# Row sums of an attention kernel: the first head's exponentials interleaved and summed on VectorE, three heads added on GpSimd

## The chip, the core and the metric

The kernel runs on one core of one Trainium2 chip. The metric is the device time of one execution in microseconds (us). Five engines work side by side and meet through semaphores: TensorE (PE, its weight loads are shown as PEld), VectorE (DVE), ScalarE (ACT), GpSimd (POOL) and SyncE (SP), which here only starts transfers.

## The reference

One block of a diffusion transformer on `x` of 2 x 2048 x 512 with a condition of 2 x 512. The condition makes six shifts, scales and gates; attention is causal over 2048 tokens with 16 heads of 32; a GELU layer of width 2048 follows.

```python
scores = jnp.einsum('bhqd,bhkd->bhqk', q, k) * scale
causal = jnp.tril(jnp.ones((t, t), bool))
scores = jnp.where(causal, scores, -jnp.inf)
attn = jax.nn.softmax(scores, axis=-1)
out = jnp.einsum('bhqk,bhkd->bhqd', attn, v)
...
mod = jax.nn.silu(condition) @ Wada + bada
sh_a, sc_a, gt_a, sh_m, sc_m, gt_m = jnp.split(mod, 6, axis=1)
xm = _layernorm(x, g1, be1) * (1.0 + sc_a[:, None, :]) + sh_a[:, None, :]
x = x + gt_a[:, None, :] * _attention(xm, Wqkv, Wproj, bproj)
xm = _layernorm(x, g2, be2) * (1.0 + sc_m[:, None, :]) + sh_m[:, None, :]
h = jax.nn.gelu(xm @ W1 + b1, approximate=False)
x = x + gt_m[:, None, :] * (h @ W2 + b2)
```

The softmax is exact: its maximum over the keys is subtracted, and its sum over the keys divides. The change concerns that sum.

## The kernel before, in words

The two rows of the batch are worked one after the other: projections to q, k and v, then attention, then the output projection; a Strassen-like multilayer stage for both rows closes the run. Everything is f32, with scores in the f32r form.

Attention of one row is cut into 16 units, `units`: four column blocks `c` of four heads each (`HC` = 4, 32 columns a head), and in each block four blocks `i` of 512 queries (`QB`, `TQ` = 4 tiles of 128). In block 0 they run in the order 0, 1, 2, 3, in the others 0, 2, 1, 3. A unit goes over its key tiles of 128 in steps: 4 i steps for tiles wholly below the diagonal, one for the first diagonal tile, one for the second and fourth together, one for the third (`steps_of`, line 662).

A step does this, in the order in which the code writes it; nearly all instructions keep that order on their engine (`mm`, `act`):

- `scores_t` (line 550): for four heads PE writes minus the row maxima into four banks (`st<-fold,sel`), adds the transposed scores, keys by queries (`st<-qst,kst`), and ACT takes the exponential of each into `e` (line 593). On diagonal tiles POOL zeroes what lies above the diagonal (line 602). There are four `st` banks.
- Between these, PE makes scores the other way round, queries by keys, for units up to three ahead (`score`, `bank`; `s<-kst,qst`), and DVE takes their row maxima (`mx`, lines 461 and, on the diagonal with a causal mask, 456). They use two `s` banks, and one score in a step borrows an `st` bank. How many are made in a step is set by `due` from fixed costs. When a unit's last maximum is there, `split` (lines 478 to 482) and `rows` (line 522) form the rows that the next unit's first matmuls need. In the last unit of a row no scores are left to make.
- `flush` runs what was put off: `values` (`o<-e,vv`) two steps later (`LAG`), and the row sums `sm`, matmuls of `e` or of a chain of sums with a matrix of ones.
- The row sums are not taken of every tile. For each group of four full key tiles the four `e` of the same head are first added, by POOL or, in the last unit of a row, by DVE (`add`, line 621), and one matmul per head then sums the result over the keys. The last group of a unit takes in the first diagonal tile as well. The other diagonal tiles go straight to PE.

The four heads of a step lie in two tiles of two heads each, so an add is one instruction of 1024 elements a partition for two heads. There is room for four steps of `e` and for two chains.

Of the kernel before, what the change touches and what calls it, by code (L numbers as in the profile page):

```python
# [8 lines left out]
F32 = mybir.dt.float32  # L9
F32R = mybir.dt.float32r  # L10
BF16 = mybir.dt.bfloat16
AF = mybir.ActivationFunctionType
ALU = mybir.AluOpType
AX = mybir.AxisListType
# [3 lines left out]
P = 128  # L18
H = 16
HD = 32  # L20
EPS = 1e-5
QB = 512
# [5 lines left out]
def dit_block_kernel(  # L28
# [36 lines left out]
    nc = tc.nc  # L65
# [5 lines left out]
    HC = P // HD  # L71
    TQ = QB // P
# [4 lines left out]
    E_BUFS = 16  # L77
    EE_BUFS = 8
# [5 lines left out]
    def pool(name, bufs=1, **kw):  # L84
# [5 lines left out]
    bp = bp_cm.__enter__()  # L90

    ident = const.tile([P, P], F32, tag="ident", name="ident")
# [2 lines left out]
    causal = bp.tile([P, QB], BF16, tag="causal", name="causal")  # L95
    nc.gpsimd.memset(causal[:, : QB - P], 0.0)
    make_causal_mask(nc, causal[:, QB - P :], mask_val=MASKED)
    ones = bp.tile([P, P], F32, tag="ones", name="ones")
    nc.gpsimd.memset(ones, 1.0)
    eps = const.tile([P, 1], F32, tag="eps", name="eps")  # L100
    nc.gpsimd.memset(eps, EPS)
# [2 lines left out]
    sel = bp.tile([P, P], BF16, tag="sel", name="sel")  # L104
    ident_h = bp.tile([P, P], BF16, tag="ident_h", name="ident_h")
    nc.vector.tensor_copy(ident_h, ident)
    nc.vector.tensor_scalar(sel, ones, -1.0, None, ALU.mult)
    tmask = bp.tile([P, TQ + 1], F32, tag="tmask", name="tmask")
    nc.vector.tensor_reduce(
        tmask[:, :TQ],  # L110
# [1 line left out]
        axis=AX.XY,  # L112
        op=ALU.add,
# [21 lines left out]
    first = const.tile([P, 1], F32, tag="first", name="first")  # L135
# [65 lines left out]
    def mm(*args, **kw):  # L201

        return tc.keep_in_program_order(nc.tensor.matmul(*args, **kw))  # L203

    def act(ins):

        return tc.keep_in_program_order(ins)
# [81 lines left out]
    class Row:  # L289


        def __init__(self, b):
            self.b = b
            self.vv = bp.tile([P, NT, D], F32, tag="vv", name="vv")
            self.kst, self.qst, self.pools = {}, {}, {0: bp}
            self.at = 0
            self.todo = [
                (u, h, t, kb)
                for u, (_, i) in enumerate(units)
                for h in range(HC)  # L300
                for t in range(TQ)
                for kb in range(i + 1)
            ]
            self.mx = None
            self.spent = 0
            self.rows_made = 0
# [234 lines left out]
    def attention_phase(row):  # L541
        b, vv, kst, qst = row.b, row.vv, row.kst, row.qst
        with pool(f"att{b}") as ap, pool(
# [2 lines left out]
            row.pools[1] = ap  # L546

            n_bank = [0]

            def scores_t(u, step, n):  # L550

                def st_bank():  # L560

                    n_bank[0] += u == len(units) - 1
                    if n_bank[0] % 6 >= HC:
                        return ps_sp.tile([P, QB], F32, tag="s", name="st")
                    return ps_stp.tile([P, QB], F32, tag="st", name="st")

                c, i = units[u]
                tiles = steps_of[u][step]
                q0 = tiles[0][1]
                w = sum(QB - q for _, q in tiles)  # L570
                sts, es = [], []
                for h in range(HC):
                    g = slice(h * HD, (h + 1) * HD)
                    st = st_bank()
                    mm(
                        st[:, :w], sel[g, :], fold[u % 2][g, q0 : q0 + w],
                        start=True, stop=False,
                    )
                    sts.append(st)
                for h in range(HC):  # L580
                    at = 0
                    for j, q in tiles:
                        mm(
                            sts[h][:, at : at + QB - q],
                            kst[c][:, h, j * P : (j + 1) * P],
                            qst[u][:, h, q:],
                            start=False, stop=at + QB - q == w,
                        )
                        at += QB - q
                    if h % 2 == 0:  # L590
                        e = ap.tile([P, 2, QB], F32, tag="e", name="e", bufs=E_BUFS // 2)
                        es.append(e)
                    act(nc.scalar.activation(e[:, h % 2, :w], sts[h][:, :w], AF.Exp))  # L593
                    if tiles[0][0] >= i * TQ and (h % 2 or len(tiles) > 1):

                        if len(tiles) > 1:
                            d = e[:, h % 2, :].rearrange("p (t k) -> p t k", k=P)
                            d = d[:, 0 : TQ : TQ - 1, :]
                        else:
                            d = e[:, :, :P]  # L600
                        act(
                            nc.gpsimd.affine_select(  # L602
                                d, d, pattern=[[0, 2], [1, P]],
                                compare_op=ALU.is_ge, fill=0.0,
                                base=0, channel_multiplier=-1,
                            )
                        )
                    if h < 2 and n >= 3 or h >= HC - n and n < 3:
                        row.score(1)
                if n >= 3:  # L610
                    row.score(1, st_bank)
                    row.score(min(n, HC) - 3)
                return es, max(0, n - HC)

            def new_sums():
                return [
                    ap.tile([P, 2, QB], F32, tag="ee", name="ee", bufs=EE_BUFS // 2)
                    for _ in range(HC // 2)
                ]

            def add(u, dst, x, y):
                engine = nc.vector if u == len(units) - 1 else nc.gpsimd
                act(engine.tensor_tensor(dst, x, y, ALU.add))  # L623

            def add_to(u, chain, es):
                for t, e in zip(chain, es):
                    add(u, t, t, e)

            def begin_chain(u, es0, es1):
                chain = new_sums()  # L630
                for t, e0, e1 in zip(chain, es0, es1):
                    add(u, t, e0, e1)
                return chain

            def products(dst, lhs, es, q0, at, first, last):
                for h in range(HC):
                    mm(
                        dst[h * HD : (h + 1) * HD, q0:], lhs(h),
                        es[h // 2][:, h % 2, at : at + QB - q0], start=first, stop=last,
                    )  # L640

            def finish(u, o, sm):
# [26 lines left out]
            for u, (c, i) in enumerate(units):  # L669
                for n, tiles in enumerate(steps_of[u]):  # L670
                    w = sum(QB - q for _, q in tiles)
# [12 lines left out]
            for u, (c, i) in enumerate(units):  # L684
# [5 lines left out]
                for n_step, tiles in enumerate(steps_of[u]):  # L690
                    last = n_step == steps - 1
                    if n_step == 0:
                        summed = set()
                        o = ps_op.tile([P, QB], F32, tag="o", name="o")
                        sm = ps_op.tile([P, QB], F32, tag="sm", name="sm")
# [6 lines left out]
                    if u == 0 and n_step < LAG:  # L702

                        n = max(n, HC)
                    es, rest = scores_t(u, n_step, n)
                    rest = len(row.todo) - rest
                    make_rows = False
# [12 lines left out]
                    def tile_by_tile(dst, lhs, es, tiles, first, last):  # L720
                        at = 0
                        for n, (j, q) in enumerate(tiles):
                            products(
                                dst, lambda h: lhs(j, h), es, q, at,
                                first and n == 0, last and n == len(tiles) - 1,
                            )
                            at += QB - q
# [8 lines left out]
                    def row_sums(es, last, tiles=((0, 0),), sm=sm, summed=summed):  # L736
                        first = not summed
                        summed.add(len(summed))
                        tile_by_tile(sm, lambda j, h: ones[:, :HD], es, tiles, first, last)

                    pending.append((now + LAG, values))
                    sums_of, wait = None, 0
                    if n_step < i * TQ:
                        k = n_step % TQ
                        if k == 0:
                            even = es
                        elif k == 1:
                            chain = begin_chain(u, even, es)
                        else:
                            add_to(u, chain, es)  # L750
                        if k == TQ - 1 and n_step + 1 < i * TQ:
                            sums_of, wait = (chain, False), 2
                    elif i and n_step == i * TQ:
                        add_to(u, chain, es)
                        sums_of, wait = (chain, False), 2
                    else:

                        sums_of, wait = (es, last, tiles), i > 0 and not last
                    if sums_of:
                        pending.append(  # L760
                            (now + LAG + wait, lambda f=row_sums, s=sums_of: f(*s))
                        )
# [304 lines left out]
    with pool("wada") as wp, pool("qkv0") as qp, pool(  # L1067
# [123 lines left out]
        with pool("hl0") as hp:  # L1191
# [8 lines left out]
            quarters.store()  # L1200

    attention_phase(row)


# [720 lines left out]
```

## Time and profile before

| | |
|---|---|
| time, median of 2 runs | 2317.93 us (2315.91 to 2319.94) |
| the profiled execution | 2323.13 us, its span 2321.4 us |
| PE busy | 2270.8 us (98%) |
| DVE busy | 1582.5 us (68%) |
| POOL busy | 1290.9 us (56%) |
| ACT busy | 914.6 us (39%) |
| granted clock of PE, mean | 0.998 |
| POOL, adds of 1024 (line 623) | 212 + 84, 2385 ns each |
| ACT, exponentials of 512 (line 593) | 1024, 603 ns each |

A profile shows one execution. Its page lists the busy time of each engine and the costliest groups of instructions: line, engine, operation, written and read tiles, shapes, count, then busy time and mean duration, then how long the engine stood idle just before them and for whom. Matmuls are pipelined, so their durations overlap and their ends are modelled; the distance from start to start tells their pace. An order of instructions lists start, duration, and in square brackets the idle time before. Attention of the first row fills some 213 to 737 us of the span, that of the second 997 to 1528.

### The profile page before, as it was taken

Reading aid. Unit: us, or ns where it says so; the run is one execution under the profiler, and the core shown is the slowest. Engines: PE = TensorE matmul, PEld = TensorE weight load, DVE = VectorE, ACT = ScalarE, POOL = GpSimd, SP = SyncE. Lnnn points to the kernel's source line nnn. Section 1 sums busy time; section 2 is a strip of 40 time slices with the busy share of each in tenths; the row PEclk is TensorE's granted clock in tenths of the full one; section 3 lists DMA queues with packets and bytes.
Section 4 is the critical chain, followed back from the end, with each engine's and each line's share of the span. In section 5 each row is a group of like instructions: output and inputs, shape, how many; then the busy total and the mean of one; then the engine's idle time right before and its main releaser. Section 6 shows DMA issues by size and latency. Waiting matters only on the chain. (4 is left out here: it accounts for less than half of the span.)

```text
span 2321.4 us, 33398 instructions
## 1 busy us (share of the span) xinstructions
PE 2270.8 (98%) x12141; PEld 1388.8 (60%) x12141; DVE 1582.5 (68%) x3117; ACT 914.6 (39%) x1744; POOL 1290.9 (56%) x1036
## 2 busy tenths in 40 slices
PE   8999999999999999999999999999999999999998
PEld 4455545455544444555455554446888888888887
DVE  3366776777666735677667777555896876877787
ACT  2112555555565021155555554622332152251230
POOL 1052987878793663478788886653764602602510
PEclk9999999999999999999999999999999999999999
DMA  7577216151233799981522404265375554654643
GB/s 257 185 243 204 55 28 133 29 119 47 74 115 127 241 297 298 320 235 24 113 48 48 100 24 134 81 206 205 118 279 200 199 186 146 212 173 151 216 143 116
DMA packets 118524, 355.60 MB, mean 153 GB/s; under 512 B 14496, under 2 KB 15052, under 8 KB 103640
## 3 DMA queue, kind: packets, MB, share of 16 engines
q1 hardware_dynamic: 107040, 293.64, 41.9%
q0 software_dynamic: 10944, 59.28, 7.0%
q8 instruction: 96, 1.57, 0.3%
q14 instruction: 68, 0.56, 0.1%
q10 hardware_dynamic: 376, 0.55, 0.1%
HBM read 253.80 MB, written 107.48 MB: 156 GB/s over the span
## 5 line engine op out<-in xcount | busy, mean ns | idle before, releaser
L593 ACT ACTIVATE e<-st 128x512 f32<-128x512 f32 (+1 forms) x1152 | 573.1, 579 | 411.6 <-PE st L203 350.5
L461 DVE TENSOR_REDUCE mx<-s 128x1 f32<-128x512 f32 x604 | 408.0, 687 | 185.0 <-PE s L203 183.6
L623 POOL TENSOR_TENSOR ee<-ee,e 128x1024 f32<-128x1024 f32 x212 | 498.8, 2385 | 8.3 <-ACT e L593 8.3
L203 PE MATMUL s<-kst,qst 128*128 128x512 f32 (+3 forms) x1032 | 466.5, 453 | 15.9 <-DVE mx L461 6.3
L203 PE MATMUL st<-qst,kst 128*128 128x512 f32 (+3 forms) x1280 | 410.1, 387 | 0.0
L203 PE MATMUL ps_a<-sum,room 128*128 128x256 f32 x1504 | 357.4, 382 | 6.6 <-DVE c L1409 3.8
L203 PEld LDWEIGHTS ps_a<-sum,room 128*128 128x128 f32 x1504 | 281.5, 190 | 56.0 <-issue 8.7
L203 PE MATMUL o<-e,vv 128*32 128x512 f32 (+3 forms) x2560 | 300.8, 539 | 0.8 <-POOL e L602 0.8
L203 PEld LDWEIGHTS s<-kst,qst 128*128 128x128 f32 x1032 | 194.5, 189 | 174.0 <-DVE mx L461 58.6
L456 DVE CUSTOM_DVE_ANT_0 junk<-s,causal 128x512 bf16<-128x512 f32 (+3 forms) x428 | 209.2, 489 | 126.2 <-PE s L203 118.7
L203 PEld LDWEIGHTS st<-qst,kst 128*128 128x128 f32 x1280 | 227.5, 188 | 96.8 <-issue 66.7
L623 POOL TENSOR_TENSOR ee<-e 128x1024 f32<-128x1024 f32 x84 | 198.4, 2384 | 130.5 <-ACT e L593 130.4
L203 PE MATMUL ps_qk<-xmT,wqkv 128*128 128x512 f32 x512 | 240.5, 597 | 1.8 <-DVE xmT L263 1.8
L602 POOL TENSOR_SCALAR_AFFINE_SELECT e<-e 128x256 f32<-128x256 f32 x256 | 103.8, 436 | 107.2 <-ACT e L593 74.2
L203 PEld LDWEIGHTS ps_qk<-xmT,wqkv 128*128 128x128 f32 x512 | 94.2, 190 | 97.7 <-issue 91.4
L1637 POOL TENSOR_TENSOR c<-c,h 128x512 f32<-128x512 f32 x40 | 58.2, 1474 | 160.8 <-ACT c L1635 160.8
L203 PE MATMUL ps_b<-sum,room 128*128 128x256 f32 x608 | 143.6, 379 | 0.0
L203 PEld LDWEIGHTS ps_b<-sum,room 128*128 128x128 f32 x608 | 115.0, 190 | 15.4
L203 PE MATMUL ps_v<-wqkv,xmT 128*128 128x512 f32 x256 | 122.3, 594 | 0.0
L203 PEld LDWEIGHTS o<-e,vv 128*32 128x32 f32 x2560 | 60.8, 108 | 101.1 <-issue 83.4
L203 PE MATMUL st<-fold,sel 32*128 32x512 bf16 (+1 forms) x1152 | 116.1, 372 | 3.6 <-DVE mhl L482 2.6
L461 DVE TENSOR_REDUCE mx<-st 128x1 f32<-128x512 f32 x164 | 112.7, 687 | 4.9 <-PE st L203 2.7
(179 smaller groups left out, 2869.6 us busy)
## 6 DMA issues: line engine op xcount, KB each, us to landing
qst<-q SPq DMA_DIRECT2D x128, 256.0 KB
room<-w1e SPq DMA_DIRECT2D x28, 1024.0 KB
kst<-k SPq DMA_DIRECT2D x24, 1024.0 KB
room<-w1e SPq DMA_DIRECT2D x28, 768.0 KB
room<-w2e SPq DMA_DIRECT2D x21, 1024.0 KB
q<-hl SPq DMA_DIRECT2D x32, 512.0 KB
k<-hl SPq DMA_DIRECT2D x32, 512.0 KB
room<-w2e SPq DMA_DIRECT2D x21, 768.0 KB
```

What stands on the lines that cost most here:

```text
L203: return tc.keep_in_program_order(nc.tensor.matmul(*args, **kw))
L456: nc.vector.tensor_tensor_reduce(junk[:, :w], s[:, :w], causal[:, QB - w :], 1.0, MASKED, ALU.add, ALU.max, m,)
L461: nc.vector.tensor_reduce(m, s[:, :w], axis=AX.X, op=ALU.max)
L593: act(nc.scalar.activation(e[:, h % 2, :w], sts[h][:, :w], AF.Exp))
L602: nc.gpsimd.affine_select(d, d, pattern=[[0, 2], [1, P]], compare_op=ALU.is_ge, fill=0.0, base=0, channel_multiplier=-1,)
L623: act(engine.tensor_tensor(dst, x, y, ALU.add))
L1637: nc.gpsimd.tensor_tensor(c, c, piece_of(base, i, t, pair), ALU.add)
```

## The change

The first of the four heads is taken out of the pairs. Its exponentials of four successive key tiles go into one tile `[P, QB, TQ]`, so that for each query the values of the four key tiles lie side by side: ACT writes them, and PE reads them, at a step of four elements (16 bytes). When the fourth is there, one `tensor_reduce` on DVE over the innermost axis gives the sum of the group for that head, 2048 elements read and 512 written. The other three heads lie side by side in one tile of 3 x 512, and each add is one instruction of 1536. In the last group of a unit, the first diagonal tile of the first head is added by an add of its own. The masking on the diagonal goes by one head and three heads instead of two and two. There is room for two groups of the first head, four steps of the others, and two chains, as before. The matrix of ones shrinks to the 32 columns that are used.

```diff
@@ scores_t and above it
+            four = [None]
+            class Heads:
+                def __init__(self, first, rest):
+                    self.first, self.rest = first, rest
+                def of(self, h):
+                    return self.rest[:, h - 1, :] if h else self.first
+            def exponentials(step):
+                if step % TQ == 0:
+                    four[0] = ap.tile([P, QB, TQ], F32, tag="e0", name="e", bufs=2)
+                return Heads(
+                    four[0][:, :, step % TQ],
+                    ap.tile([P, HC - 1, QB], F32, tag="e", name="e", bufs=E_BUFS // HC),
+                )
...
-                sts, es = [], []
+                sts, es = [], exponentials(step)
...
-                    if h % 2 == 0:
-                        e = ap.tile([P, 2, QB], F32, tag="e", name="e", bufs=E_BUFS // 2)
-                        es.append(e)
-                    act(nc.scalar.activation(e[:, h % 2, :w], sts[h][:, :w], AF.Exp))
-                    if tiles[0][0] >= i * TQ and (h % 2 or len(tiles) > 1):
+                    e = es.of(h)
+                    act(nc.scalar.activation(e[:, :w], sts[h][:, :w], AF.Exp))
+                    if tiles[0][0] >= i * TQ and (h in (0, HC - 1) or len(tiles) > 1):
...
             def add_to(u, chain, es):
-                for t, e in zip(chain, es):
-                    add(u, t, t, e)
+                add(u, chain.rest, chain.rest, es.rest)
             def begin_chain(u, es0, es1):
-                chain = new_sums()
-                for t, e0, e1 in zip(chain, es0, es1):
-                    add(u, t, e0, e1)
+                chain = Heads(
+                    ap.tile([P, QB], F32, tag="ee0", name="ee", bufs=2),
+                    ap.tile([P, HC - 1, QB], F32, tag="ee", name="ee", bufs=2),
+                )
+                add(u, chain.rest, es0.rest, es1.rest)
                 return chain
+            def four_of_first(chain):
+                act(
+                    nc.vector.tensor_reduce(
+                        chain.first, four[0], axis=AX.X, op=ALU.add,
+                    )
+                )
             def products(dst, lhs, es, q0, at, first, last):
...
-                        es[h // 2][:, h % 2, at : at + QB - q0], start=first, stop=last,
+                        es.of(h)[:, at : at + QB - q0], start=first, stop=last,
...
-                        if k == TQ - 1 and n_step + 1 < i * TQ:
-                            sums_of, wait = (chain, False), 2
+                        if k == TQ - 1:
+                            four_of_first(chain)
+                            if n_step + 1 < i * TQ:
+                                sums_of, wait = (chain, False), 2
                     elif i and n_step == i * TQ:
                         add_to(u, chain, es)
+                        add(u, chain.first, chain.first, es.first)
                         sums_of, wait = (chain, False), 2
```

More of the change, by code (lines that the diff above doesn't have):

```diff
@@ L97, in dit_block_kernel @@
     make_causal_mask(nc, causal[:, QB - P :], mask_val=MASKED)
-    ones = bp.tile([P, P], F32, tag="ones", name="ones")
+    ones = bp.tile([P, HD], F32, tag="ones", name="ones")
     nc.gpsimd.memset(ones, 1.0)
@@ L106, in dit_block_kernel @@
     nc.vector.tensor_copy(ident_h, ident)
-    nc.vector.tensor_scalar(sel, ones, -1.0, None, ALU.mult)
+    nc.vector.tensor_scalar(sel, ident, 0.0, -1.0, ALU.mult, ALU.add)
     tmask = bp.tile([P, TQ + 1], F32, tag="tmask", name="tmask")
@@ L589, in scores_t @@
                         at += QB - q
-                    if h % 2 == 0:
-                        e = ap.tile([P, 2, QB], F32, tag="e", name="e", bufs=E_BUFS // 2)
-                        es.append(e)
-                    act(nc.scalar.activation(e[:, h % 2, :w], sts[h][:, :w], AF.Exp))
-                    if tiles[0][0] >= i * TQ and (h % 2 or len(tiles) > 1):
-                        if len(tiles) > 1:
-                            d = e[:, h % 2, :].rearrange("p (t k) -> p t k", k=P)
-                            d = d[:, 0 : TQ : TQ - 1, :]
+                    e = es.of(h)
+                    act(nc.scalar.activation(e[:, :w], sts[h][:, :w], AF.Exp))
+                    if tiles[0][0] >= i * TQ and (h in (0, HC - 1) or len(tiles) > 1):
+                        if h == 0 or len(tiles) > 1:
+                            d = e.rearrange("p (t k) -> p t k", k=P)
+                            d = d[:, 0 : TQ : TQ - 1, :][:, : len(tiles), :]
                         else:
-                            d = e[:, :, :P]
+                            d = es.rest[:, :, :P]
                         act(
                             nc.gpsimd.affine_select(
-                                d, d, pattern=[[0, 2], [1, P]],
+                                d, d, pattern=[[0, d.shape[1]], [1, P]],
                                 compare_op=ALU.is_ge, fill=0.0,
@@ L613, in scores_t @@
                 return es, max(0, n - HC)
[L615 to L619, printed above, removed]
             def add(u, dst, x, y):
@@ L625, in add_to @@
             def add_to(u, chain, es):
-                for t, e in zip(chain, es):
-                    add(u, t, t, e)
+                add(u, chain.rest, chain.rest, es.rest)
             def begin_chain(u, es0, es1):
-                chain = new_sums()
-                for t, e0, e1 in zip(chain, es0, es1):
-                    add(u, t, e0, e1)
-                return chain
+                chain = Heads(
[3 more added lines that the diff above has]
+                add(u, chain.rest, es0.rest, es1.rest)
+                return chain
+            def four_of_first(chain):
+                act(
+                    nc.vector.tensor_reduce(
+                        chain.first, four[0],
+                        axis=AX.X, op=ALU.add,
+                    )
+                )
             def products(dst, lhs, es, q0, at, first, last):
@@ L738, in row_sums @@
                         summed.add(len(summed))
-                        tile_by_tile(sm, lambda j, h: ones[:, :HD], es, tiles, first, last)
+                        tile_by_tile(sm, lambda j, h: ones, es, tiles, first, last)
                     pending.append((now + LAG, values))
```

## The prediction

> **What bounds the kernel now.** I read the page's first part, then the busy table of the four attention stretches (both rows of the batch, without their last unit; then one long unit; then a last unit), then the groups by shape, the waits and the order of instructions. The columns of the busy table are stretch, length, busy time and count for PE, PEld, DVE, ACT and POOL, then the granted clock and the DMA's share and rate.
>
> ```profile
> span 2321.4 us, 33398 instructions
> PE 2270.8 (98%) x12141; PEld 1388.8 (60%) x12141; DVE 1582.5 (68%) x3117; ACT 914.6 (39%) x1744; POOL 1290.9 (56%) x1036
> 213.45:693.84 480.39, 474.08 (x3308) 241.71 (x3308) 335.74 (x840) 272.01 (x545) 388.07 (x262) 1.00 0.33 80
> 996.93:1484.29 487.36, 476.87 (x3308) 242.64 (x3308) 340.28 (x844) 271.94 (x545) 392.14 (x266) 1.00 0.33 84
> 291.02:336.80 45.78, 45.78 (x308) 22.68 (x305) 32.49 (x83) 26.00 (x50) 38.67 (x20) 1.00 0.12 29
> 1484.29:1527.50 43.21, 42.26 (x307) 16.91 (x304) 30.82 (x30) 31.23 (x63) 10.85 (x13) 1.00 0.19 68
> ```
>
> PE sets the pace: it idles 6.3 us in 480.4 and 10.5 in 487.4, at the full granted clock. POOL is busy for 81% of these stretches, DVE for 70%, and in the long unit (third row) for 84% and 71%. So whatever the change takes from POOL can bring at most what PE now loses on account of POOL. That is small:
>
> ```profile
> DVE mx L461 <- PE s L203: 183.6, 279, 2.8
> ACT e L593 <- POOL ee L623: 15.1, 10, 1.7
> ```
>
> All waits of ACT for POOL are 15.1 us in the whole run, and ACT idles for hundreds more. PE's own matmuls wait 0.8 us for POOL's masking (a row further down) and show none for its sums. What PE does lean on is DVE: each score matmul `s` needs one of two banks that DVE's maximum frees. One group of four key tiles in the long unit shows it, PE's rows first, then DVE's (start, length):
>
> ```profile
> 307.06 0.49 PE L203 MATMUL s<-kst,qst 128*128 128x512 f32 x1
> 308.15 0.39 PE L203 MATMUL s<-kst,qst 128*128 128x512 f32 x1
> 308.37 0.39 PE L203 MATMUL st<-qst,kst 128*128 128x512 f32 x1
> 308.60 0.34 PE L203 MATMUL s<-kst,qst 128*128 128x384 f32 x1
> 309.48 0.39 PE L203 MATMUL s<-kst,qst 128*128 128x512 f32 x1
> 309.80 1.07 PE L203 MATMUL o<-e,vv 128*32 128x512 f32 x8
> 310.80 0.40 PE L203 MATMUL st<-fold,sel 32*128 32x512 bf16 x4
> 307.59 0.69 DVE L461 TENSOR_REDUCE mx<-s 128x1 f32<-128x512 f32 x1 [0.51 <-PE s L203]
> 308.57 0.69 DVE L461 TENSOR_REDUCE mx<-s 128x1 f32<-128x512 f32 x1 [0.29 <-PE s L203]
> ```
>
> The step's last score is issued at 307.06 and DVE has its maximum by 308.28. DVE idles 0.29 us and reduces the score of 308.15 by 309.26. PE writes the same bank again at 309.48, only 0.22 us later. DVE is thus not full, but the slack at each bank is tenths of a microsecond.
>
> **The change, part by part.** Durations come from these rows (last numbers before the second bar: busy us, mean ns):
>
> ```profile
> L623 POOL TENSOR_TENSOR ee<-ee,e 128x1024 f32<-128x1024 f32 x212 | 498.8, 2385 | 8.3 <-ACT e L593 8.3
> L461 DVE TENSOR_REDUCE mx<-s 128x1 f32<-128x512 f32 x604 | 408.0, 687 | 185.0 <-PE s L203 183.6
> L478 DVE TENSOR_REDUCE s<-mx 128x16 f32<-128x64 f32 x6 | 1.4, 228 | 0.2
> L478 DVE TENSOR_REDUCE s<-mx 128x16 f32<-128x48 f32 x8 | 1.7, 208 | 0.2
> L479 DVE TENSOR_REDUCE mhl<-mx 128x16 bf16<-128x48 f32 x8 | 1.6, 196 | 0.0
> ```
>
> *Count.* Per column block `c` the units have 0+1+2+3 groups of four full key tiles; four blocks and two rows make 48 groups. The last unit of each row (3 groups each) has no scores left to make, so 42 groups run beside scores.
>
> *POOL.* Six adds of 1024 per group (6 x 2.385 = 14.3 us) become three of 1536 (3 x 2.385 x 1.5 = 10.7 us), 3.6 us less per group, 150 us of POOL's time. The diagonal tile's 4.8 us become 3.6 and an add of 512 (1.2): nothing. The masking stays two operations a step. Worth to the end: between 0 and the 15.1 us of ACT's waits. I take 4, since ACT's idle time hides most of them.
>
> *DVE, the new reduction.* It reads 2048 elements and writes 512. From 64 to 512 elements the reductions above grow by (687 - 228)/448 = 1.025 ns an element, and sixteen short results cost nothing beyond their elements, so I estimate 228 + 1984 x 1.025 = 2262 ns, say 2.27 us. It is issued at the end of the group's fourth step, behind all maxima of that step, and the next step's maxima queue behind it. In the group above it would start at 308.28 and end at 310.55. The maximum of 308.57 would then end at 311.24, and the score of 309.48, which needs that bank, waits 1.8 us. Behind it in PE's order stand the values of the step before last and the masks of the next step (309.80, 310.80), so the whole chain slides. DVE then runs without gaps and the next use of a bank costs nothing more. The other group of this unit, at its eighth step:
>
> ```profile
> 322.54 0.40 PE L203 MATMUL s<-kst,qst 128*128 128x512 f32 x1
> 323.82 0.28 PE L203 MATMUL s<-kst,qst 128*128 128x256 f32 x1
> 322.03 0.19 DVE L482 TENSOR_TENSOR mhl<-s,mhl 128x16 bf16<-128x16 f32 x1
> 322.98 0.69 DVE L461 TENSOR_REDUCE mx<-s 128x1 f32<-128x512 f32 x1 [0.76 <-PE s L203]
> ```
>
> Here the reduction runs from 322.22 to 324.49, the maximum ends at 325.18 and the score of 323.82 (the second after it) waits 1.4 us. Bounds per group: 0 (all in DVE's idle time) and 2.27 (none). The middle of the two groups, 1.6, is also what the waits give: DVE's mean idle stretch before a maximum is 183.6/279 = 0.66 us, and 2.27 - 0.66 = 1.61. I take 1.6: 42 x 1.6 = 67 us, with bounds 0 and 95.
>
> *DVE in the last units.* There DVE adds, and no bank of PE's waits for it. The 6 adds of 1024 become three of 1536 and a reduction.
>
> ```profile
> L623 DVE TENSOR_TENSOR ee<-ee,e 128x1024 f32<-128x1024 f32 x28 | 35.2, 1294 | 5.0 <-ACT e L593 3.7 <-POOL e L602 1.2
> ```
>
> That is 7.8 us against 3 x 1.9 + 2.27 = 8.1, beside 43.2 us of PE: nothing. The cover gone, it would cost 0.3 us a group.
>
> *ACT's writes and PE's reads at a step of 16 bytes.* The first head's exponentials are written, and read by the value and row-sum matmuls, with three foreign elements between two of their own. No row here shows such an access.
>
> ```profile
> L593 ACT ACTIVATE e<-st 128x512 f32<-128x512 f32 x1024 | 530.9, 603 | 365.5 <-PE st L203 306.8 <-PE s L203 39.6 <-POOL ee L623 13.4
> L593 ACT ACTIVATE e<-st 128x256 f32<-128x256 f32 x128 | 42.2, 383 | 46.2 <-PE st L203 43.7 <-POOL ee L623 1.7
> L203 PE MATMUL o<-e,vv 128*32 128x512 f32 x1792 | 238.8, 605 | 0.0
> L203 PE MATMUL o<-e,vv 128*32 128x384 f32 x256 | 33.9, 498 | 0.8 <-POOL e L602 0.8
> L203 PE MATMUL sm<-e,ones 128*32 128x384 f32 x256 | 27.7, 486 | 0.0
> L203 PE MATMUL sm<-e,ones 128*32 128x512 f32 x64 | 8.3, 592 | 0.0
> 308.40 2.06 ACT L593 ACTIVATE e<-st 128x512 f32<-128x512 f32 x4 [1.50 <-PE st L203]
> ```
>
> For ACT the lower bound is 0, the upper one every element twice: (603 - 383)/256 = 0.86 ns an element, +0.44 us for the first head. ACT's four take 2.06 us and end at 310.46, the masks that need the last bank start at 310.80, so 0.34 us is free and +0.44 costs about 0.1 to 0.16 us a step, 26 to 41 us over 258 steps (1024 + 128 exponentials make 288 steps of four, less the 30 of the last units). The nearest row for a scattered write is DVE's `mhl` (every fourth two-byte element): 196 ns against 208 for the same input written in one piece. So I take 0, keeping 41.
>
> For PE the lower bound is 0: eight value matmuls, two rounds of four side by side, take 309.80 to 310.80, about 0.43 us more for each round of 512 (605 against 498 for 384 is 107 per 128), while the two 512-wide matmuls of 308.15 and 308.37 above are followed by the next after 0.22 and 0.23 us, so PE can fetch f32 twice as fast as the value matmuls need it. Upper bound: each such round twice as long. Head 0's columns: (1792 x 512 + 256 x (384 + 256 + 128))/4 for `o` and (64 x 512 + 256 x 768)/4 for `sm` (the narrower forms also count 256) are 336,000, or 656 rounds of 512, times 0.43 = 282 us. I take 0, by the spare fetch rate just named, and keep 282.
>
> [...]
>
> *Sum.* 2323.13 (the profiled execution, 1.7 us beyond its span) - 4 + 67 = 2386; it stands 5 us above the median of the runs shown, 2317.93, so I forecast **2382 us**.
>
> **The rivals.**
>
> *First, not slower:* POOL's relief is the term that counts and the reduction falls into DVE's idle time. Place: the long units, where POOL is busy 38.67 of 45.78 us and DVE idle for 13.3. Three reductions take 6.8 of these 13.3. Price: 0 for the reduction and all 15 us of ACT's waits back, 2318 - 15 = 2303. It decides if DVE finds idle stretches over 2.27 - 0.2 us where the reduction stands; for it speaks the longest such wait (2.8 us), against it their mean of 0.66.
>
> *Second, slower on ACT:* the scattered write takes +0.44 us. PE then waits for the last head's bank in many steps; 2382 + 33 = 2415. The last units would show it first: 31.23 busy of 43.21 there, in steps that ACT nearly fills. For it: ACT must touch a new place per element. Against: the `mhl` row.
>
> *Third, far slower on PE:* the value and row-sum matmuls of head 0 take twice as long, +282. Steps then grow by 0.86 us, four of them by 3.4, which is more than the reduction, so its 67 falls to about 10: 2318 + 282 + 10 = 2610. For it: four streams are fetched side by side there, and one would need four times its places. Against: the spare rate above.
>
> *Fourth, not what it says:* if the interleaved slices of one tile are taken as overlapping, ACT's next exponential waits for POOL's masking of the slice before, behind 3.6 us adds; at some 1.4 us in each of 30 units, 2382 + 42 = 2424.
>
> **How the numbers follow.** Forecast 0.55 (own range 2345 to 2425), first rival 0.14, second 0.10, third 0.17, fourth 0.04. A measurement of this kernel tells about 2%, 46 us, from no change: 2271.6 to 2364.3. Faster by more needs PE's idle time in attention, 16.8 us, three times over: 0.03, out of the first rival. Within 2%: the rest of the first (0.11) and the forecast's low end, under 1.2 us a group (0.09), 0.20. Slower: 0.77. The range runs from 2335 (0.5 us a group) to 2620, since without the third rival more than 2 in 10 would be left out.
>
> **What would show it.** Right: a DVE reduction of about 2.27 us 48 times; score matmuls with PE idle, or late, behind `mx` after each; PE's stretches above longer by some 33 us each; POOL's busy time down by 150. The exponential of head 0 at 603 ns and `o` at 605 clear the second and third rival; 1.0 us and 0.9 us or more prove them. The forecast is wrong if those stretches keep their length, or if they grow evenly in every step rather than after each fourth one.

## The result and the profile after

The changed kernel takes 2713.94 us (median of 2, 2708.12 to 2719.76) against 2317.93: 1.1703 times as long, interval 1.165 to 1.1755. I had forecast slower, 2382 us with a range up to 2620; the time lies 94 us above that range.

The first part of the page of the changed kernel, then its busy table, with the columns of the prediction's, for both rows without their last unit, the long unit and the first row's last unit. The first row's last unit before, which the prediction does not show, stands at the end.

```profile
span 2706.4 us, 32982 instructions
PE 2630.0 (97%) x12141; PEld 1392.2 (51%) x12141; DVE 1683.3 (62%) x3147; ACT 1029.4 (38%) x1744; POOL 1167.9 (43%) x910
212.96:876.14 663.18, 640.31 (x3308) 243.49 (x3307) 385.31 (x861) 322.59 (x545) 327.13 (x202) 1.00 0.24 58
1191.58:1857.26 665.68, 642.76 (x3309) 245.34 (x3309) 387.82 (x865) 322.81 (x545) 327.85 (x203) 0.99 0.24 61
317.76:381.24 63.48, 61.34 (x305) 22.51 (x305) 36.93 (x83) 30.98 (x50) 30.25 (x9) 1.00 0.08 18
876.14:930.60 54.46, 53.57 (x288) 16.04 (x288) 31.32 (x23) 36.38 (x58) 8.11 (x9) 1.00 0.15 53
...
693.84:734.94 41.10, 40.15 (x290) 15.99 (x287) 28.79 (x29) 29.64 (x59) 8.73 (x11) 1.00 0.21 72
```

The two stretches grew from 480 and 487 us to 663 and 666. DVE's share there fell from 70% to 58%, POOL's from 81% to 49%. PE issues as many matmuls as before (12141) and yet is busy 359 us longer. So the time is not a wait for the new reduction alone: matmuls themselves became longer. The last two rows say it most plainly. In a last unit no scores are made whose bank a late reduction could hold back, and it went from 41.1 us to 54.5. The groups by shape after the change (those before are in the prediction):

```profile
L610 ACT ACTIVATE e<-st 128x512 f32<-128x512 f32 x1024 | 637.7, 730 | 582.5 <-PE st L203 560.5 <-PE s L203 17.3 <-issue 3.4
L203 PE MATMUL o<-e,vv 128*32 128x512 f32 x1792 | 453.8, 730 | 0.0
L634 POOL TENSOR_TENSOR ee<-ee,e 128x1536 f32<-128x1536 f32 x106 | 370.5, 3496 | 147.4 <-ACT e L610 145.5
L650 DVE TENSOR_REDUCE ee<-e 128x512 f32<-128x2048 f32 x48 | 109.3, 2278 | 0.0
```

The reduction takes 2278 ns, 2.27 us as estimated, and POOL's add 3496 instead of 2 x 2385. But `o`, unchanged in number and width, went from 605 to 730 ns, and ACT's exponential from 603 to 730. If one head in four carries all of it (for PE, `e10_pe_only` below shows that it does), that is 4 x 125 ns = 0.50 us more for a matmul of head 0 and 4 x 127 ns = 0.51 us for its exponential. The exponentials of head 0 at 335.92, 340.87, 346.90 and 886.58 take 1.09, 1.10, 1.07 and 1.12 us; before, those at 322.80, 707.79 and 720.11 take 0.60. The order of PE's work in a last unit, before and then after, shows what that does:

```profile
704.48 0.40 PE L203 MATMUL st<-fold,sel 32*128 32x512 bf16 x4
704.80 1.20 PE L203 MATMUL st<-qst,kst 128*128 128x512 f32 x4
705.93 1.06 PE L203 MATMUL o<-e,vv 128*32 128x512 f32 x8
706.93 0.40 PE L203 MATMUL st<-fold,sel 32*128 32x512 bf16 x4
...
885.71 0.39 PE L203 MATMUL st<-fold,sel 32*128 32x512 bf16 x4
886.04 1.20 PE L203 MATMUL st<-qst,kst 128*128 128x512 f32 x4
887.17 2.03 PE L203 MATMUL o<-e,vv 128*32 128x512 f32 x8
889.13 0.40 PE L203 MATMUL st<-fold,sel 32*128 32x512 bf16 x4
```

Masks and scores keep their 1.45 us. The eight value matmuls, two rounds for four heads side by side, went from 1.00 us (705.93 to 706.93) to 1.96. What comes next starts when the slowest head is nearly done, the one whose operand lies at a step of 16 bytes: in a step of `e10_pe_only` the six matmuls of the other heads are over at 338.01 (336.95 and 1.06), head 0's second at 338.95 (337.87 and 1.08), and the next masks start at 338.88.

### The profile page after: what moved, and what is told of

Its sections match the earlier page's. It is cut to its first block, busy times and chain, and to the rows that moved or that the text cites. A ratio compares the mean times of both kernels' runs of the same rounds, so it can differ in the third digit from the quotient of the medians.

```text
span 2706.4 us, 32982 instructions
## 1 busy us (share of the span) xinstructions
PE 2630.0 (97%) x12141; PEld 1392.2 (51%) x12141; DVE 1683.3 (62%) x3147; ACT 1029.4 (38%) x1744; POOL 1167.9 (43%) x910
## 4 chain that ended last, share of the span: by engine, by line
PE 85%; DVE 7%; ACT 4%; issue 3%; DMA 1%; ACTq 0%; DVEq 0%; SPq 0%
PE o L203 19%; PE st L203 15%; PE ps_a L203 12%; PE s L203 8%; PE ps_qk L203 7%; PE ps_b L203 6%; PE sm L203 6%; PE ps_v L203 4%; PE ps_o L203 4%; ACT e L610 3%; PE ps_c L203 3%; DVE sum L1311 1%; DVE ee L650 1%; PE ps_xt L211 1%; DVE h L1433 1%
## 5 line engine op out<-in xcount | busy, mean ns | idle before, releaser
L610 ACT ACTIVATE e<-st 128x512 f32<-128x512 f32 (+1 forms) x1152 | 684.7, 700 | 640.7 <-PE st L203 618.2
L203 PE MATMUL o<-e,vv 128*32 128x512 f32 (+3 forms) x2560 | 565.4, 647 | 0.0
L634 POOL TENSOR_TENSOR ee<-ee,e 128x1536 f32<-128x1536 f32 (+1 forms) x128 | 403.8, 3162 | 147.4 <-ACT e L610 145.5
L634 POOL TENSOR_TENSOR ee<-e 128x1536 f32<-128x1536 f32 x42 | 146.8, 3495 | 369.1 <-ACT e L610 369.1
L619 POOL TENSOR_SCALAR_AFFINE_SELECT e<-e 128x256 f32<-128x256 f32 (+2 forms) x256 | 122.1, 499 | 220.9 <-ACT e L610 220.2
L203 PEld LDWEIGHTS <-sel 32*128 32x128 bf16 x1152 | 29.4, 91 | 270.1 <-issue 265.8
L203 PE MATMUL sm<-e,ones 128*32 128x384 f32 (+3 forms) x832 | 143.5, 468 | 0.0
L203 PEld LDWEIGHTS o<-e,vv 128*32 128x32 f32 x2560 | 67.9, 109 | 120.9 <-issue 100.6
L203 PE MATMUL st<-kst,qst 128*128 128x512 f32 (+1 forms) x248 | 114.6, 462 | 13.5 <-ACT e L610 3.2
```

Of the source, the lines that this page charges most:

```text
L610: act(nc.scalar.activation(e[:, :w], sts[h][:, :w], AF.Exp))
L619: nc.gpsimd.affine_select(d, d, pattern=[[0, d.shape[1]], [1, P]], compare_op=ALU.is_ge, fill=0.0, base=0, channel_multiplier=-1,)
```

## The experiments

My theory after this: every engine pays for the step of 16 bytes, and the reduction costs what it costs besides. The rival: the split of the sum over two engines is at fault, the layout innocent. Times are medians. Every ratio is to the kernel before, run on the same chip beside them (medians 2321.34, 2320.13 and 2321.96 us in three sets).

**The layout undone, the split kept (`e1_apart`).**

```diff
-                    four[0] = ap.tile([P, QB, TQ], F32, tag="e0", name="e", bufs=2)
+                    four[0] = ap.tile([P, TQ, QB], F32, tag="e0", name="e", bufs=2)
...
-                    four[0][:, :, step % TQ],
+                    four[0][:, step % TQ, :],
...
-                        chain.first, four[0],
+                        chain.first, four[0].rearrange("p t q -> p q t"),
```

> The first head's four key tiles lie one after the other, so that ACT writes and PE reads them without gaps, and VectorE's reduction reads at a step of 2 KB instead; the order of all engines is that of the changed kernel. Theory of the step (a 16-byte step costs ACT and PE about twice the time per element): the 512-wide round of head 0 falls from 0.95 us to the 0.43 to 0.45 of the other heads, its exponential from 1.09 to 0.60 us, and what is left is the reduction, 42 x 1.6 us: about 2385 us if the reduction stays at 2.28 us, about 2470 if VectorE pays for its own step. Rival (the split of the sum over two engines costs the time, the layout does not): about 2700 us, with head 0's matmuls still long.

2480.68 us, 1.0682 times before (1.0644 to 1.072). 233 us are gone, so the rival's 2700 is out. The exponential is back at 600 ns. What is left is near the 2470 that the forecast gave for the case that VectorE pays for its own step, and that is what happened:

```profile
L650 DVE TENSOR_REDUCE ee<-e 128x512 f32<-128x2048 f32 x48 | 181.7, 3786 | 0.0
213.77:771.83 558.06, 502.30 (x3310) 254.62 (x3310) 410.86 (x861) 276.89 (x545) 315.42 (x199) 0.95 0.28 69
323.89 0.50 PE L203 MATMUL s<-kst,qst 128*128 128x512 f32 x1 [2.96 <-DVE mx L461]
324.31 1.64 PE L203 MATMUL o<-e,vv 128*32 128x512 f32 x8
```

3786 ns instead of 2278. And the granted clock over the first row's attention is 0.95 instead of 1.00: after a wait of 2.96 us for DVE the next value matmuls take 1.64 us instead of 1.06. The masks behind them take 0.61 us instead of 0.39. That the wait itself brings the lower clock was not shown. Against the next run, without the reduction, PE is idle for 56 us of the stretch instead of 6 and busy for 502 instead of 474.

**The reduction taken out of that (`e2_apart_nosum`)**, by `chain.first = es.first` in place of the `tensor_reduce`.

> As e1_apart, and VectorE's reduction is left out: the row sum of the first head takes the last of four key tiles alone. Theory of the step: nothing is left but GpSimd's relief, 2305 to 2325 us; the difference to e1_apart is the price of the reduction, 60 to 70 us if my 1.6 us a group hold. Rival (GpSimd was the bound): below 2290.

2319.75 us, ratio 0.9992 (0.9981 to 1.0003). This is GpSimd's relief alone, and its worth cannot be told from nothing:

```profile
214.73:694.92 480.19, 473.92 (x3309) 242.51 (x3309) 335.63 (x840) 275.24 (x545) 314.16 (x199) 1.00 0.33 80
```

POOL is busy 314 us instead of 388 in a stretch that stays at 480.2 us. The profiled execution took 2333.13 us, above the median of the eleven: its second row's stretch lasted 502.61 us, at a clock of 0.98. That there is no gain rests on the median and not on this row. The difference to `e1_apart` is 161 us, not the 60 to 70 of the forecast, which had not counted VectorE's own step and the clock.

**The reduction alone, without a step on any engine (`e8_reduce_v`).**

```diff
-                        chain.first, four[0].rearrange("p t q -> p q t"),
+                        chain.first,
+                        vv[:, :TQ, :].rearrange("p n (q t) -> p (n q) t", t=TQ),
```

> As e1_apart, but VectorE's reduction reads 2048 adjacent elements of v in place of the exponentials, so that no engine has a step: the reduction at 2.28 us in its place in the queue, alone. By my prediction's 1.6 us for each of 42 groups: 67 us over e2_apart_nosum (2320), 2380 to 2395. Rival (it falls into VectorE's idle time): under 2340. What e3_act_scatter (2426) has over it is then the price of ACT's step, some 35 to 45 us.

2374.00 us, 1.0234 (1.0204 to 1.0263): 54 us for 42 groups, 1.3 us a group, a little below the forecast. A small part of it is, by estimate, a lower clock in the second row: 0.98 in the profiled execution, with PE busy for 485.37 us where the first row has 478.26 at 1.00. The group that the prediction worked out by hand, PE's rows and then DVE's:

```profile
315.18 0.39 PE L203 MATMUL st<-kst,qst 128*128 128x512 f32 x1
317.05 0.51 PE L203 MATMUL s<-kst,qst 128*128 128x512 f32 x1 [1.49 <-DVE mx L461]
314.12 2.27 DVE L650 TENSOR_REDUCE ee<-vv 128x512 f32<-128x2048 f32 x1
316.32 0.68 DVE L461 TENSOR_REDUCE mx<-s 128x1 f32<-128x512 f32 x1
```

The score that followed the borrowed one after 0.23 us before (309.25 to 309.48) now follows after 1.87. The step lasts 5.08 us instead of 3.32: 1.76 more, where 1.8 was forecast. At the eighth step it is 4.91 us instead of 3.58: 1.33 more, where 1.4 was forecast.

**PE's step alone (`e10_pe_only`)**: the layout of `e1_apart`, no reduction, and head 0's matmuls read `v` at a step of four elements in place of the exponentials.

```diff
-                        es.of(h)[:, at : at + QB - q0], start=first, stop=last,
+                        (es.of(h) if h else es.read)[:, at : at + QB - q0], start=first, stop=last,
...
+                    vv.rearrange("p n d -> p (n d)")[:, 0 : 4 * QB : 4],
```

> PE's step alone: ACT writes without gaps, VectorE's reduction is left out, PE's value and diagonal row-sum matmuls of head 0 read v at a step of 16 bytes (the chain's row sums read v without gaps). If the step's price is 656 rounds of 0.95 instead of 0.45 us and nothing hides it: 2320 + 328, about 2645. If half of it lies beside waits that the kernel had anyway: about 2480.

2610.48 us, 1.1261 (1.1226 to 1.1295): 288.5 us, between the two forecasts and nearer to the one in which nothing hides the step.

```profile
L203 PE MATMUL o<-vv 128*32 128x512 f32 x448 | 452.3, 1099 | 0.0
L203 PE MATMUL o<-e,vv 128*32 128x512 f32 x1344 | 236.6, 603 | 0.0
```

Head 0's matmuls stand here by themselves: 1099 ns against 603 for the three heads beside it. Nothing writes what they read, so it is PE's own step. 656 rounds of 0.50 us would be 328. From start to start the two rounds of a step take 1.95 us on the mean of the first row's attention (1.93 in the step at 336.95), 0.99 before; that is 0.48 a round and 315 in all. PE's idle time in the two long stretches fell from 17 to 10 us. Some 20 us stay open.

**ACT's step alone (`e11_act_only`)**: the layout of the changed kernel, no reduction, and head 0's matmuls read `v` without gaps.

> ACT's step alone: ACT writes head 0's exponentials at a step of 16 bytes, PE reads v without gaps in their place, VectorE's reduction is left out. If ACT's price is its own and adds to the reduction's (e3_act_scatter less e8_reduce_v is 52 us): about 2372. If it only shows together with a late VectorE: under 2335.

2389.87 us, 1.0295 (1.0277 to 1.0313): 68 us, above the 2372 of the forecast, so ACT's price is its own. The waits and the group of the borrowed score say where; the last row is that group before:

```profile
PEld st L203 <- ACT e L612: 98.7, 209, 0.6
L203 PE MATMUL st<-kst,qst 128*128 128x512 f32 x188 | 92.3, 491 | 11.5 <-ACT e L612 3.4
...
L203 PE MATMUL st<-kst,qst 128*128 128x512 f32 x188 | 75.6, 402 | 0.0
```

The borrowed score takes the bank of head 0 of the same step, the first that ACT gives back. With an exponential of 1.1 us (1.07 to 1.12 in the changed kernel, above) it is given back too late: the weight load waits for ACT 209 times, 0.47 us each, where the kernel before has 12 such waits with 2.1 us in all. The changed kernel has the same 209 (98.9 us). Weight loads overlap matmuls (in the first row's 514.70 us PE is busy for 501.72 and its weight loads for 236.42), so PE does not lose all of that. In the step worked out by hand the borrowed score starts 0.71 us after the scores ahead of it (316.00 to 316.71), 0.47 before (308.78 to 309.25): 0.24 us, or 50 us for 209 such steps. The matmuls of that group take 491 ns, 402 before. With the reduction as well (`e3_act_scatter`) it is 2426.49 us, 1.0466 (1.0443 to 1.0488): 105 us, where 54 and 68 add up to 122. The time lies in the range of the forecast, but 54 us below `e1_apart`, not above it as the forecast's reasoning had it, since that kernel pays for VectorE's step and this one does not.

> The changed kernel, but PE's matmuls of head 0 read a fixed run of v without gaps in place of the exponentials; ACT still writes at a step of 16 bytes and VectorE still reduces. Theory of the step: exponential of head 0 at 1.09 us, matmul rounds back at 0.43 to 0.45; 30 to 75 us over e1_apart (first head's bank is late for the borrowed score), so 2415 to 2460. Rival (ACT's longer write is hidden): equal to e1_apart.

**The changed kernel without the reduction (`e6_inter_nosum`, `e12_inter_nosum`).** The second mends the first, in which 24 chains' sums of head 0 were read at a step that the changed kernel does not have there.

> The changed kernel with VectorE's reduction left out (the row sum of the first head takes the last of four key tiles alone): the step of ACT and PE stays. Two theories on the reduction in the longer steps. Prediction's third rival (a step longer by 0.9 us covers it, 10 us are left): 2700. Other (what is queued behind the reduction comes as late as before, since the step grows behind the last maximum and not in front of it): 60 us or more below the changed kernel, 2640 to 2655.

> The changed kernel without VectorE's reduction, as e6_inter_nosum, but the chain's row sums of head 0 read v without gaps, so that leaving the reduction out adds no step of its own (in e6 24 of the chains' sums were read at a step of 16 bytes, some 24 us). About 2680, so that the reduction is worth some 33 us in the changed kernel: between the 10 of my third rival and the 54 that it costs alone. If PE's and ACT's prices add up without overlap: e10 + e11 less 2320, about 2697.

2705.06 us, 1.167 (1.1643 to 1.1698), and 2681.73 us, 1.1567 (1.1535 to 1.1598). The first lies near the 2700 of the third rival, but only because of that step. The 360 us of the second are within 4 us of the 288 of PE and the 68 of ACT. The reduction is worth 32 us in the changed kernel (2713.94 - 2681.73; 36 if each is taken over the kernel before that ran beside it). Its order shows that the longer steps cover it in some groups and not in others; the group at the fourth step, then the one at the eighth:

```profile
339.58 0.50 PE L203 MATMUL s<-kst,qst 128*128 128x512 f32 x1
343.65 0.49 PE L203 MATMUL s<-kst,qst 128*128 128x512 f32 x1 [1.14 <-DVE mx L461]
340.72 2.28 DVE L650 TENSOR_REDUCE ee<-e 128x512 f32<-128x2048 f32 x1
...
359.07 2.02 PE L203 MATMUL o<-e,vv 128*32 128x512 f32 x8
360.29 2.28 DVE L650 TENSOR_REDUCE ee<-e 128x512 f32<-128x2048 f32 x1
363.36 0.28 PE L203 MATMUL s<-kst,qst 128*128 128x256 f32 x1
```

At the fourth step a last score (339.58) stands behind the value matmuls. DVE reduces only after it, and the longer values lie in front of the reduction, not beside it: 1.14 us of PE's idle time are left, and the step lasts 6.03 us (340.01 to 346.04) where the one before it, without a reduction, lasts 4.95. At the eighth step the reduction begins while the values still run. That step lasts 4.94 us (361.02 to 365.96), no longer than one without a reduction.

**The length of the step (`e4_pe_step2`, `e4_pe_step3`, `e4_pe_step4`, `e5_pairs`).** The first three are `e1_apart` with head 0's matmuls reading `v` at a step of 8, 12 and 16 bytes; ACT has no step, and the first two were timed once.

> As e4_pe_step4 with a step of 8 bytes for PE's reads. [...]

> [...]

> As e1_apart, but PE's matmuls of head 0 read v at a step of four elements, 16 bytes, in place of the exponentials; ACT writes without gaps. Theory of the step: rounds of head 0 at 0.95 us, 656 of them 0.5 us longer: 320 us over a kernel without, 2640 to 2700. [...]

2474, 2597 and 2717.55 us (the last 1.1711, 1.1693 to 1.173), against 2481 without a step on PE. Their matmuls of head 0, in this order:

```profile
L203 PE MATMUL o<-vv 128*32 128x512 f32 x448 | 267.6, 679 | 0.0
...
L203 PE MATMUL o<-vv 128*32 128x512 f32 x448 | 361.0, 892 | 0.0
...
L203 PE MATMUL o<-vv 128*32 128x512 f32 x448 | 452.6, 1100 | 0.0
```

The other heads take 634, 644 and 628 in these kernels, where 603 were measured above at a clock of 0.999; a part of that is, by estimate, the lower clock (0.981, 0.979 and 0.986). So head 0 takes 45, 248 and 472 ns more. At 8 bytes the addition is small. At 12 bytes the addition is about half of that at 16. The kernel with 16 bytes lies 237 us over `e1_apart`, less than the 288 of PE's step alone; PE's waits for the maxima fell from 107 to 88 us there, and the rest was not traced. In the changed kernel itself a step of 8 bytes comes from interleaving two by two:

```diff
-                    four[0] = ap.tile([P, QB, TQ], F32, tag="e0", name="e", bufs=2)
+                    four[0] = ap.tile([P, 2, QB, 2], F32, tag="e0", name="e", bufs=2)
...
-                    four[0][:, :, step % TQ],
+                    four[0][:, step % TQ // 2, :, step % 2],
...
-                        chain.first, four[0],
-                        axis=AX.X, op=ALU.add,
+                        chain.first, four[0].rearrange("p a q b -> p q a b"),
+                        axis=AX.XY, op=ALU.add,
```

> The changed kernel with the first head's key tiles interleaved two by two instead of four by four: ACT writes and PE reads at a step of 8 bytes, VectorE reads runs of two. [...] If any step costs: ACT near 0.8 to 1.1 us, rounds near 0.9, 2550 to 2714.

2385.85 us, 1.0295 (1.0272 to 1.0317), 12 us over the reduction alone and far under the 2550 of the forecast for a step that costs:

```profile
L610 ACT ACTIVATE e<-st 128x512 f32<-128x512 f32 x1024 | 538.4, 608 | 420.4 <-PE st L203 406.7 <-PE s L203 10.2 <-issue 2.0
L203 PE MATMUL o<-e,vv 128*32 128x512 f32 x1792 | 256.3, 616 | 0.0
L650 DVE TENSOR_REDUCE ee<-e 128x512 f32<-128x2048 f32 x48 | 109.3, 2277 | 0.0
```

ACT, PE and DVE are all near their first durations. Nothing in these runs points to a version faster than the kernel before, since the relief that the change brings is worth nothing that could be measured.

## Why the prediction was wrong, point by point

- **The bound.** Right: PE sets the pace, and taking work from POOL brings nothing (4 us taken; 2 measured, within the noise). POOL's busy time fell by 123 us, not by 150.
- **PE's reads: the step that failed.** I took 0 of bounds 0 and 282, "by the spare fetch rate". Measured alone: 288, a little above even the upper bound. The spare rate was seen on operands without gaps, where each 16 bytes hold four elements. PE gets through a score's 512 columns in 0.22 us and through a value's in 0.43 (from two widths), twice the pace in elements, but at a step of 16 bytes an operand spreads over four times the bytes. If the spare rate is one of bytes gone over, which is my estimate and not shown, four times the bytes at twice the pace would be a round twice as long, which is about what came (0.98 us from start to start instead of 0.50). The row was right and its unit, by that estimate, wrong. At two elements to 16 bytes head 0's matmuls took 679 ns, at one 1100.
- **ACT's writes.** I took 0 of bounds 0 and 41, by the reduction that writes every fourth two-byte element. Measured alone: 68, also above the bound. That row had sixteen results and a step of 8 bytes, and a step of 8 bytes costs ACT next to nothing here too (`e5_pairs`, 608 ns on the mean instead of 603). The bound was low because I looked at the masks' wait for the last head, and the wait that came was the borrowed score's for the first.
- **The reduction.** Taken 67 us, measured 54 alone. Place, duration and the two hand-worked groups were right (1.76 and 1.33 us where 1.8 and 1.4 were forecast). The mean of 1.3 says that other groups cost less; which ones was not traced.
- **Combination.** The rivals were priced one at a time. PE's and ACT's steps have one cause and came together. The bounds that I had, 282 and 41, with the 67 make 2318 + 390 = 2708, 6 us from the result. That closeness is luck: 41 was too low by 27, and the 67 became 32 in the longer steps. The three prices measured alone make 288 + 68 + 54 = 410, of which 396 appeared. In the third rival the reduction was to fall to about 10. The range ended at 2620 because it left room for that rival alone, at 2610, and not for ACT's step on top of it. The stated sum also comes to 2381 rather than 2382, which changes nothing.
- **What was to show it.** The signs named for the third rival (a mean of 0.9 us or more for `o`, meant as head 0's) were there: 1.1 us. So was a sign that the forecast is wrong, steps that grow without a reduction in them: 3.56 us before (303.92 to 307.48), 4.95 after (335.06 to 340.01). Of the first rival there is no sign, and of the fourth none either, since the changed kernel's waits show none of ACT for POOL.

## What to carry to other kernels

Price a changed layout at every engine that touches it, by the step between its elements and not by their number alone: here an instruction took 1.7 times as long on DVE at a step of 2 KB (3786 ns against 2278), and at 16 bytes 1.8 times on ACT (1.07 to 1.12 us against 0.60) and PE (1099 ns against 603), but at 8 bytes little more than without gaps (PE 679 ns against 634). When several unknown prices hang on one cause, add their upper bounds for the end of the range. And before moving work off a busy engine, ask whether anyone waits for it; an experiment that only drops the work answers that.

## What the runs showed of the hardware that was not expected

At a step of 16 bytes or more three engines came to nearly one rate, by estimates from the measured times. PE's round: 0.84 ns an element without gaps (0.43 us for 512), plus (1099 - 603)/512 = 0.97, makes 1.81 ns. In `e10_pe_only` 512 columns take 1099 ns and 384 take 875, which gives 1.75. DVE, whose step was 2 KB: 3786/2048 = 1.85 against 1.11. ACT: 0.86 from its two widths, plus 0.51 us for 512, makes about 1.86. Score matmuls, 512 elements without gaps in 0.23 us, take 1.8 ns for every four elements. PE's steps of 8 and 12 bytes gave 0.84 + 45/512 = 0.93 and 0.84 + 248/512 = 1.32 ns an element, against 0.90 and 1.36 for half and three quarters of 1.81. So in these runs an element alone in its 16 bytes took about as long as four adjacent elements of a score, for one stream of reads or writes. It can't be one limit on all reads together: without gaps the eight value matmuls of a step, four side by side, read 8 x 512 elements in 1.00 us, less than 1 ns for every four. Why three engines come to the same figure was not shown. A step of more than 16 bytes was tried on DVE alone, and two such streams side by side were not tried.

The clock was the other surprise. In `e1_apart` the granted clock was 0.95 over the attention of both rows, with 31 waits of PE for the maxima of line 461 (68.7 us, the longest 3.4) and 19 for those of line 456 (38.4 us, the longest 2.8) in the whole run. In `e8_reduce_v`, with 27 such waits for line 461 (32.1 us, the longest 2.1), it was 1.00 in the first row and 0.98 in the second. Which waits bring it, if any, was not shown.
